# Decoder self attention on one core: four key blocks of each of 22 units are transposed by VectorE and a DRAM round trip instead of by TensorE, and the steps of the units around them are put in other orders

## The chip, the cores and the metric

One core of a Trainium2 chip runs the whole program. The metric is the device time of one execution in microseconds (us), the median of several runs. All data is float32.

The engines are named as in the profile: PE is TensorE (matrix multiplications and transposes), PEld its loading of weights, DVE is VectorE, ACT is ScalarE, POOL is GpSimd, SP is SyncE, which here only issues DMA transfers. Each engine works through its own list of instructions in order, and waits on semaphores that other engines or transfers raise.

## The reference

The program is one encoder layer over a short context (2 batches of 77 rows) and one decoder layer over `x` (2 batches of 2048 rows), 512 channels, 16 heads of 32 channels. The change concerns the causal self attention of the decoder alone:

```
yn = _ln(y, dec_n1_s, dec_n1_b)
q, k, v = heads of yn @ w.T + b                      # 16 heads of 32
scores = einsum('bhqd,bhkd->bhqk', q, k) / sqrt(32)
scores = scores + bias[None]                         # relative bias, -inf above the diagonal
attn = softmax(scores, axis=-1)
out = einsum('bhqk,bhkd->bhqd', attn, v)
y = y + out @ w_out.T + b_out
```

Behind it come cross attention over the encoder's output and a feed-forward part of width 2048. The relative bias is constant for keys that lie 127 and more behind the query, and drops out of the softmax there, so only the last two key blocks of a row take a bias.

## The kernel before, in words

The 2048 query rows of a batch `b` are cut into four blocks `m` of 512, a block into four tiles `t` of 128; the 16 heads are cut into four groups `g` of four heads. A **unit** is `(b, m, g, t)`: one tile of 128 queries for four heads `r`. It attends to `4 m + t + 1` key blocks `k` of 128 keys. "Second blocks" are the units with `m == 1`: 16 in each batch, with 5 to 8 key blocks, so that the first four key blocks are those of `m == 0`.

What is done for a unit:

- `scores`: for a piece of up to four key blocks, four matmuls (L375), one a head, write 128 queries by up to 512 keys to PSUM. The four run side by side, since each uses 32 rows of the array. VectorE moves them to the SBUF tile `pp` and takes the maximum of each row on the way (L384; with the bias for the last two key blocks L391). Behind the last piece VectorE reduces the maxima to `nm` (L401) and puts four exponentials on a list.
- `exps(1)` lets ScalarE do the next exponential of that list (L406): one for each head, over all key blocks of the unit.
- `turn`: the probabilities lie with the queries on the partitions, and the next product needs the keys there. For one key block, PE transposes four 128 by 128 tiles (L417, one a head) into one PSUM bank, and ScalarE (L423) or VectorE (L421) copies the bank to one of the eight places of the SBUF tile `pts`.
- `values`: for each key block four matmuls (L441) with the transposed probabilities as the moving operand and `vv` as weights, side by side, summed up in one PSUM bank; when the unit is closed, ScalarE copies the sum to `oT` (L454), or VectorE adds it there (L456) where the unit was summed in two parts.

The order is written out by hand. For each unit with `m > 0` there is a string of steps, which the loop over the units plays: `a` and `d` turn the next key block (with the copy on ScalarE or VectorE), `E` is one exponential of the unit that comes next, `S` the next piece of scores (of a unit up to two further on), `v` and `V` the value products of what is turned so far (`V` closes the sum), `j` and `J` a part or all of the work that other stages of the program put in between (projections, the encoder, cross attention; their PE lines are L1120, L1035, L576, L584, L748, L305, L797, L852, L860, L869). In the kernel before there are 24 strings, one for each `(b, m, t)`, the same for all four `g`. Before a unit's string starts, whatever is left of its scores and exponentials is done.

`pp` holds two units at a time, one from either end. `held_by` says which unit holds which place of it; a piece of scores may be written when its places are free, which they are when their key block has been turned.

All transfers are issued by SP, in the order of the program: loads of weights into three `wqk` buffers (L1104, L1024), large loads into `vv` (L531), rows of `x`, the bias. An issue waits for the buffer that it overwrites, and what is behind it waits too.

Of the kernel before, what the change touches and what calls it, by code (L numbers as in the profile page):

```python
# [17 lines left out]
P = 128  # L18
# [36 lines left out]
def tile_encoder_decoder(ctx: ExitStack, tc: tile.TileContext, ins, out):  # L55
# [103 lines left out]
    with (  # L159
# [17 lines left out]
        count = {"pts": 0, "oT": 0, "mm": 0}  # L177
# [178 lines left out]

        def scores(n, k0, kn):
# [23 lines left out]
            for r in range(HC):  # L381
                p, s, c = st["p"][r], banks[r].rearrange("p (k x) -> p k x", x=P), col
                if far:
                    nc.vector.tensor_scalar(  # L384
                        p[:, k0 : k0 + far], s[:, :far], 1.0, None, ALU.mult, ALU.max,
                        accum_out=st["mx"][:, r, c : c + 1],
                    )
                    c += 1
# [23 lines left out]
        def turn(load, by):  # L412

            pt = bank()
            pts = in_turn("pts", pts_all).rearrange("p (x q) -> p x q", q=P)
# [13 lines left out]
        def values(n, ks, ends, closes):  # L429
# [9 lines left out]
            for k in ks:  # L439
                for r in range(HC):  # L440
                    nc.tensor.matmul(  # L441
                        ot[rows4(r)], vv[:, k, ts(g * HC + r, HD)], got.pop((n, k, r)),
                        start=k == ks[0] and (whole or not begun), stop=k == ks[-1] and (whole or not keep),
                    )
# [1280 lines left out]
        def cross(x):  # L1725
# [127 lines left out]
        turned_to, scored_to, at = {n: 0 for n in range(end)}, {n: 0 for n in range(end)}, [0]  # L1853
        held_by = {}


        SCRIPTS = {
# [24 lines left out]
        }  # L1882

        def script_of(n):

            b, m, g, t = units[n]
            if n < end - 2:
                return SCRIPTS[b, m, t].split()
# [15 lines left out]
        def may_score(ahead=0):  # L1904

            if at[0] + ahead >= len(stream):
                return False
            n, k0, kn = stream[at[0] + ahead]
# [133 lines left out]
```

## Time and profile before

| | |
|---|---|
| median of 3 runs | 2707.5 us (2707.0 to 2708.48) |
| the profiled execution | 2708.39 us; its span 2706.3 us |
| PE busy | 2684.3 us, 99% of the span |
| DVE, ACT, POOL busy | 1848.9, 1526.2, 1002.3 us |
| granted TensorE clock | 0.998 |
| DMA | 385.10 MB, mean 142 GB/s |

Busy time of PE is the time in which at least one matmul is under way, and matmuls overlap: the mean of one (276 ns for a transpose) is its passage through the array, not what it adds. What one adds is read from the starts of neighbouring rows of the timeline. The second blocks lie between 160 and 372 us in the first batch and between 975 and 1165 us in the second. In the trace a float32 matmul makes two records, a transpose one; the program's order, shown below, counts instructions.

### The profile page before, as it was taken

To read this page: it belongs to the slowest core of one execution; us is meant where nothing else is said; L and a number is where in the kernel's file an instruction comes from. 1 tells how busy PE (TensorE), PEld (TensorE's weight loads), DVE (VectorE), ACT (ScalarE), POOL (GpSimd) and SP (SyncE) were. 2 spreads that over 40 slices of the span, in tenths; PEclk is the share of its full clock that TensorE was granted. 3 is DMA by queue.
4 is the path that set the end of the run, shared out by engine and by line. 5 is a ranking of instruction groups with operands and counts; after the bars stand their busy time and mean duration, and the time that the engine had idled before them with its cause. 6 is when DMAs were issued, how large, how long until landed. Compare 5 with 4: busy or idle time off the path is not lost.

```text
span 2706.3 us, 68257 instructions
## 1 busy us (share of the span) xinstructions
PE 2684.3 (99%) x26606; PEld 2199.2 (81%) x26606; DVE 1848.9 (68%) x5448; ACT 1526.2 (56%) x2960; POOL 1002.3 (37%) x844
## 2 busy tenths in 40 slices
PE   9999999999999999999999999999999999999998
PEld 6678777777776677778777887999999898989898
DVE  4776688888885687788888883737464746464635
ACT  3545567767886557777767794444443444444431
POOL 2602235500300513223300103556565555556546
PEclk9999999999999999999999999999999999999999
DMA  8734445511213522343311216565658565657575
GB/s 235 215 99 131 128 146 174 169 59 43 64 49 87 144 80 81 111 126 118 107 53 40 73 59 196 176 211 172 215 169 241 172 215 171 215 170 216 153 222 186
DMA packets 296276, 385.10 MB, mean 142 GB/s; under 512 B 41184, under 2 KB 165648, under 8 KB 295826
## 3 DMA queue, kind: packets, MB, share of 16 engines
q1 hardware_dynamic: 295954, 380.73, 46.9%
q8 instruction: 211, 3.46, 0.5%
q14 instruction: 111, 0.91, 0.1%
HBM read 334.15 MB, written 46.47 MB: 141 GB/s over the span
## 4 chain that ended last, share of the span: by engine, by line
PE 96%; DVE 1%; ACT 1%; DMA 1%; POOL 1%; SPq 0%; issue 0%; DVEq 0%; POOLq 0%; ACTq 0%
PE psum L417 18%; PE psum L1636 15%; PE psum L1665 13%; PE psum L375 11%; PE psum L441 9%; PE psum L1120 8%; PE psum L1799 3%; PE psum L1756 3%; PE psum L1035 3%; PE psum L852 2%; PE psum L822 1%; PE psum L860 1%; PE psum L576 1%; PE psum L797 1%; PE psum L239 1%; PE psum L215 1%
## 5 line engine op out<-in xcount | busy, mean ns | idle before, releaser
L406 ACT ACTIVATE pp<-pp,nm 128x128 f32<-128x128 f32 (+15 forms) x512 | 611.4, 1200 | 23.4 <-DVE nm L401 23.2
L384 DVE TENSOR_SCALAR_CACHE_REDUCE pp<-psum 128x512 f32<-128x512 f32 (+3 forms) x1024 | 556.7, 590 | 69.2 <-PE psum L375 67.1
L423 ACT COPY pts<-psum 128x512 f32<-128x512 f32 x696 | 374.4, 593 | 346.3 <-PE psum L417 309.5
L417 PE MATMUL psum<-ident,pp 128*128 128x128 f32 x4352 | 527.4, 276 | 5.7 <-ACT nT L310 4.0
L417 PEld LDWEIGHTS psum<-ident,pp 128*128 128x128 f32 x4352 | 475.2, 141 | 64.5 <-issue 21.4
L441 PEld LDWEIGHTS psum<-pts,vv 128*32 128x32 f32 x8704 | 225.7, 110 | 119.4 <-DVE pp L384 49.3
L375 PE MATMUL psum<-kT,q 32*128 32x512 f32 (+3 forms) x2560 | 320.3, 565 | 2.2 <-ACT kT L231 1.4
L421 DVE COPY pts<-psum 128x512 f32<-128x512 f32 x392 | 257.7, 686 | 84.8 <-PE psum L417 81.3
L1665 PE MATMUL psum<-pp 128*128 128x128 f32 x2560 | 304.5, 276 | 1.9 <-POOL pp L948 1.6
L1665 PEld LDWEIGHTS psum<-pp 128*128 128x128 f32 x2560 | 296.3, 192 | 8.6 <-issue 2.8
L441 PE MATMUL psum<-pts,vv 128*32 128x128 f32 x8704 | 278.0, 275 | 1.1 <-DVE pp L384 0.8
L948 POOL TENSOR_TENSOR pp<-pp 128x512 f32<-128x512 f32 x159 | 212.8, 1355 | 110.2 <-ACT pp L800 45.4
L1636 PE MATMUL psum<-vv,pp 128*128 128x256 f32 x1024 | 236.2, 381 | 0.0
L1636 PEld LDWEIGHTS psum<-vv,pp 128*128 128x128 f32 x1024 | 190.3, 190 | 25.8 <-issue 0.5
L391 DVE CUSTOM_DVE_ANT_0 pp<-psum,bias 128x256 f32<-128x256 f32 (+1 forms) x512 | 196.0, 411 | 13.2 <-PE psum L375 12.7
L375 PEld LDWEIGHTS psum<-kT,q 32*128 32x128 f32 x2560 | 127.5, 183 | 87.3 <-issue 50.0
L1649 DVE TENSOR_TENSOR kT<-kT,psum 128x512 f32<-128x512 f32 x96 | 65.8, 686 | 191.1 <-PE psum L1636 190.9
L1652 ACT ACTIVATE kT<-kT,vecs 128x256 f32<-128x256 f32 x192 | 86.9, 501 | 156.6 <-DVE kT L1649 155.9
L1636 PE MATMUL psum<-nT,pp 128*128 128x256 f32 x768 | 174.1, 380 | 0.0
L1636 PEld LDWEIGHTS psum<-nT,pp 128*128 128x128 f32 x768 | 144.2, 190 | 20.3 <-issue 1.6
L1673 ACT COPY oT<-psum 128x128 f32<-128x128 f32 x56 | 15.0, 268 | 239.1 <-PE psum L1665 239.1
L480 POOL TENSOR_TENSOR oT<-rirows,oT 128x512 f32<-128x512 f32 x30 | 38.4, 1279 | 288.6 <-DMA rirows<-rec 267.0
(272 smaller groups left out, 4108.2 us busy)
## 6 DMA issues: line engine op xcount, KB each, us to landing
pp<-w_d SPq DMA_DIRECT2D x520, 256.0 KB
pp<-in_dec_ff_wT_dram SPq DMA_DIRECT2D x112, 256.0 KB
bias<-tzg SPq DMA_DIRECT2D x128, 128.0 KB
pp<-wo_d SPq DMA_DIRECT2D x56, 256.0 KB
wqk<-in_dec_sa_in_wT_dram SPq DMA_DIRECT2D x52, 256.0 KB
wqk<-sa_q SPq DMA_DIRECT2D x84, 128.0 KB
vv<-in_enc_ff_wT_dram SPq DMA_DIRECT2D x8, 1024.0 KB
xr<-in_x_dram SPq DMA_DIRECT2D x32, 256.0 KB
```

Of the source, the lines that this page charges most:

```text
L375: nc.tensor.matmul(banks[r][:, : kn * P], q[rows4(r), ts(t, P)], kT[rows4(r), g, k0 * P : (k0 + kn) * P], start=True, stop=True,)
L384: nc.vector.tensor_scalar(p[:, k0 : k0 + far], s[:, :far], 1.0, None, ALU.mult, ALU.max, accum_out=st["mx"][:, r, c : c + 1],)
L391: nc.vector.tensor_tensor_reduce(p[:, k0 + far : i + 1], s[:, far:kn], near[:, 2 - (kn - far) :], 1.0, LOWEST, ALU.add, ALU.max, accum_out ...
L406: nc.scalar.activation(p, p, AF.Exp, bias=nm, accum_out=to)
L417: nc.tensor.transpose(pt[:, ts(x, P)], state[n]["p"][r][:, k], ident)
L421: nc.vector.tensor_copy(pts[:, : len(load), :], pt[:, :w])
L423: nc.scalar.copy(pts[:, : len(load), :], pt[:, :w])
L441: nc.tensor.matmul(ot[rows4(r)], vv[:, k, ts(g * HC + r, HD)], got.pop((n, k, r)), start=k == ks[0] and (whole or not begun), stop=k == ks ...
L948: engine.tensor_tensor(out, a, b, ALU.subtract)
L1120: nc.tensor.matmul(mm[:, ts(f, TOK)], left[:, c, ts(f, P)], right[:, c, :], start=c == 0, stop=c == 1,)
L1636: nc.tensor.matmul(mm[:, ts(f, TOK)], a[:, c, ts(f, P)], b[:, c, :], start=fresh and f == 0 and c == 0, stop=c == 1, skip_group_check=True,)
L1665: nc.tensor.matmul(psum[:, bank_i, ts(col, P)], lhs[:, c, :], w[:, c, :], start=fresh and k in (0, 3) and c == 0, stop=c == 3, skip_group_ ...
```

## The change

For the units whose string has a `D` in it, key blocks 0 to 3 are no longer turned by PE. There are eleven such units in each batch, 22 together: all second blocks with `t` of 1, 2 and 3 except `(g, t) = (0, 1)`. For them:

- `scores` writes the first piece (key blocks 0 to 3) into `pp` with its columns in another order, the 32-column quarters `a` outermost.
- `move_out`: when all four exponentials of the unit are done, VectorE transposes the 32 by 32 squares of those four key blocks in place, in two instructions of 128 by 1024, and behind each SP issues a transfer of 512 KB to a DRAM tile (`turn0` and `turn1` in turns).
- `move_in`: four transfers of 256 KB read it back, each into 32 partitions of the upper four places of `pts`. Moving the quarters does the rest of the transpose. Where a string has `O` and `I`, these are done during the unit before, when its state allows; otherwise at the unit's start.
- `D` puts the four landed key blocks at the head of those whose values are summed next. In `values`, the moving operand is then read in four runs of 32 elements that lie 2 KB apart.
- The other key blocks of such a unit are turned by PE as before, and use the lower four places of `pts`.

The strings are now one for each `(b, m, g, t)`. Those of `m == 2` and `m == 3` are the ones of before, four times each; those of `m == 1` all differ. `may_score` no longer asks how far the unit two earlier has been turned (the places of `held_by` say it), and `S` may take a later piece of a unit first.

```diff
+        SCRIPTS = {
...
+            (0, 1, 0, 1): 'a a a a j a E S J E a O E I S V O S O I',
+            (0, 1, 0, 2): 'd d a J E S E D S S O E E I V',
...
+            (1, 1, 2, 0): 'J d S d a a d E E O S E V S O E I S I O',
+            (1, 1, 2, 1): 'a J D a O S E E V E S I',
...
+        def move_out(n):
+
+            area = far_part(n)
+            for a in (0, 2):
+                two = area[:, a : a + 2].rearrange("p a c -> p (a c)")
+                nc.vector.transpose(two, two)
+                nc.sync.dma_start(bounce[n % 2][a : a + 2].rearrange("a p c -> p a c"), area[:, a : a + 2])
+
+        def landed(n):
+            return pts_all[:, HC : 2 * HC, :] if units[n][1] == 1 else far_part(n)
+
+        def move_in(n):
+
+            for a in range(HC):
+                nc.sync.dma_start(landed(n)[rows4(a)], bounce[n % 2][a].rearrange("(a q) c -> q a c", q=RB))
+
+        def moved_tiles(n):
+            parts = landed(n).rearrange("p a (r k x) -> p r k a x", r=HC, x=RB)
+            got.update({(n, k, r): parts[:, r, k] for k in range(HC) for r in range(HC)})
+            return list(range(HC))
...
+                    to, got_s = p[:, k0 : k0 + far], s[:, :far]
+                    if k0 == 0 and moved(n):
+                        to = to.rearrange("p a (k x) -> p a k x", x=RB)
+                        got_s = got_s.rearrange("p k (a x) -> p a k x", x=RB)
...
-            to_turn = list(range(size[n]))
+            if moved(n) and n not in gone:
+                gone.add(n)
+                move_out(n)
...
+            if moved(n) and n not in come:
+                come.add(n)
+                move_in(n)
+            far = HC if moved(n) else 0
+            to_turn = list(range(far, size[n]))
...
+                elif step == "O" and n + 1 < end and moved(n + 1) and n + 1 not in gone:
+                    if scored_to[n + 1] == size[n + 1] and not any(u == n + 1 for u, _ in late_exps):
+                        gone.add(n + 1)
+                        move_out(n + 1)
...
+                elif step == "D":
+                    turned[:0] = moved_tiles(n)
+                    far = 0
```

Three places in the order of the instructions, before and after. The line numbers of the changed kernel differ: scores are L507 there, turns L555, values L580, the exponential L542, copies of a sum to `oT` L594, copies to `pts` L561, the 32 by 32 transposes L473, the transfers out L474 and in L482. Lines ahead of the new functions keep their numbers (L205, L305), and those behind `turn` are the ones of before plus 140 (L1120 is L1260, L1035 L1175, L576 L716, L860 L1000, L1024 L1164, L531 L671).

**First place: PE around the first moved unit, `(0, 1, 0, 2)`.** Before, from the values of the unit ahead of it (24 matmuls, six key blocks) to its own (28, seven key blocks):

```order
L441 MATMUL psum<-pts,vv 32x128 x24
L417 MATMUL psum<-ident,pp 128x128 x24
L375 MATMUL psum<-kT,q 128x256 x4
L417 MATMUL psum<-ident,pp 128x128 x4
L1035 MATMUL psum<-nT,wqk 128x256 x2
L1035 MATMUL psum<-xt,wqk 128x256 x2
L576 MATMUL psum<-pp,vv 128x154 x16
L375 MATMUL psum<-kT,q 128x384 x4
L441 MATMUL psum<-pts,vv 32x128 x28
```

The same stretch now:

```order
L580 MATMUL psum<-pts,vv 32x128 x24
L555 MATMUL psum<-ident,pp 128x128 x12
L1175 MATMUL psum<-nT,wqk 128x256 x2
L1175 MATMUL psum<-xt,wqk 128x256 x2
L716 MATMUL psum<-pp,vv 128x154 x16
L507 MATMUL psum<-kT,q 128x256 x4
L507 MATMUL psum<-kT,q 128x384 x4
L580 MATMUL psum<-pts,vv 32x128 x28
```

Of 28 transposes 12 are left, those of the unit's three last key blocks; the rest stands as before in nearly the same order. The first 16 of the 28 value matmuls take the moved blocks, so they are the first instructions that need them.

**Second place: ACT and SP at the same unit.** ACT now, from the first exponentials of the moved unit (they span seven key blocks, 7x128) to those of the next unit:

```order
L542 ACTIVATE pp,sums<-pp,nm 128x7x128 x2
L561 COPY pts<-psum 128x512
L542 ACTIVATE pp,sums<-pp,nm 128x7x128
L594 COPY oT<-psum 128x128
L542 ACTIVATE pp,sums<-pp,nm 128x7x128
L561 COPY pts<-psum 128x512
L542 ACTIVATE pp,sums<-pp,nm 128x8x128 x4
```

SP now, from the loads ahead of the two transfers out to the next unit's four transfers in (before, the rows with `turn` were not there):

```order
L1164 DMA wqk<-sa_q 128x256 x4
L676 DMA pp<-in_rows_dram 77x512
L474 DMA turn_109<-pp 128x2x512 x2
L482 DMA pts<-turn_109 32x4x512 x4
L1164 DMA wqk<-sa_q 128x256 x2
L205 DMA wbig<-in_dec_sa_out_wT_dram 128x4x512
L671 DMA vv<-in_enc_ff_wT_dram 128x4x512
L474 DMA turn_110<-pp 128x2x512 x2
L482 DMA pts<-turn_110 32x4x512 x4
```

The copy of a sum to `oT` (L594) is that of the unit ahead, and needs its last value matmul. The fourth exponential of the moved unit stands behind it, and the transposes on VectorE wait for that exponential. On SP the six transfers stand in one row, ahead of loads that were issued without them before.

**Third place: PE at `(1, 1, 2, 1)`,** from the values of the unit ahead (20) to its own (24). Before:

```order
L441 MATMUL psum<-pts,vv 32x128 x20
L305 MATMUL psum<-ident,xt 128x128 x4
L860 MATMUL psum<-kT,pp 32x128 x16
L417 MATMUL psum<-ident,pp 128x128 x24
L375 MATMUL psum<-kT,q 128x512 x4
L441 MATMUL psum<-pts,vv 32x128 x24
```

Now:

```order
L580 MATMUL psum<-pts,vv 32x128 x20
L507 MATMUL psum<-kT,q 128x512 x4
L555 MATMUL psum<-ident,pp 128x128 x4
L305 MATMUL psum<-ident,xt 128x128 x4
L1000 MATMUL psum<-kT,pp 32x128 x16
L555 MATMUL psum<-ident,pp 128x128 x4
L507 MATMUL psum<-kT,q 128x512 x4
L580 MATMUL psum<-pts,vv 32x128 x24
```

Here 16 transposes are gone, and a piece of scores has moved up to stand right behind the values of the unit ahead. On VectorE the four moves of that piece out of PSUM stand ahead of the two transposes of the moved unit.

More of the change, by code (lines that the diff above doesn't have):

```diff
@@ L414, in turn @@
             pt = bank()
-            pts = in_turn("pts", pts_all).rearrange("p (x q) -> p x q", q=P)
+            halved = moved(load[0][0]) and units[load[0][0]][1] == 1
+            pts = in_turn("half", pts_all[:, :HC]) if halved else in_turn("pts", pts_all)
+            pts = pts.rearrange("p (x q) -> p x q", q=P)
             for x, (n, k, r) in enumerate(load):
@@ L1904, in may_score, with pick @@
         def may_score(ahead=0):
[L1906 removed]
+            if ahead >= len(stream):
                 return False
[L1908 to L1914 removed]
+            return not any(k in held_by for k in places(*stream[ahead]))
+        def pick(upto):
+            u = stream[0][0] if stream else end
+            rest = [k for k, p in enumerate(stream[:5]) if p[0] == u]
+            if not stream or u > upto:
+                return None
+            if moved(u):
+                rest.sort(key=lambda k: stream[k][1] == 0)
+            elif stream[0][1] == 0 and len(rest) > 1 and may_score():
+                rest[:2] = rest[1::-1]
+            elif not may_score():
+                return None
+            return next((k for k in rest if may_score(k)), None)
         def score_next(ahead=0):
[L1917 removed]
+            n, k0, kn = stream.pop(ahead)
             scores(n, k0, kn)
@@ L1955, in tile_encoder_decoder @@
                     turned.append(k)
-                    assert len(turned) <= pts_all.shape[1]
+                    assert sum(k >= HC or not moved(n) for k in turned) <= (HC if moved(n) and m == 1 else 2 * HC)
                     leave(n, k)
@@ L1972, in tile_encoder_decoder @@
                     feed(turned_to[n])
[L1973 removed]
+            assert not (to_turn or turned or parts or far), (n, to_turn, turned, len(parts), far)
         xt_ring += [sb.tile([P, D], F32, name="xt", tag="xt", bufs=2) for _ in range(2)]
```

57 lines of the change are left out of this document (35 added, 22 removed), and 116 rows, old and new, of the table SCRIPTS.

## The prediction

> **What bounds the kernel now.** I read first the page's busy times and the chain of work that ended last, then the windows over the two stretches of second blocks, then the timeline of PE there.
>
> ```profile
> PE 2684.3 (99%) x26606; PEld 2199.2 (81%) x26606; DVE 1848.9 (68%) x5448; ACT 1526.2 (56%) x2960; POOL 1002.3 (37%) x844
> PE 96%; DVE 1%; ACT 1%; DMA 1%; POOL 1%; SPq 0%; issue 0%; DVEq 0%; POOLq 0%; ACTq 0%
> 160.00:372.00 212.00, 211.51 (x2151) 167.85 (x2150) 150.81 (x533) 114.81 (x240) 50.29 (x41) 1.00 0.40 123
> 975.00:1165.00 190.00, 190.00 (x2042) 146.67 (x2041) 143.62 (x492) 130.41 (x275) 55.60 (x47) 1.00 0.33 96
> ```
>
> The chain is PE for 96%. In the windows the columns are length, then busy time of PE, PEld, DVE, ACT, POOL, the clock, the DMA share and GB/s. In the second blocks PE idles 0.5 us of 402, DVE is at 71% and 76%, the DMA engines at 40% and 33%. So any PE work removed there shortens the program at once, and any new wait of PE lengthens it at once: nothing hides either. Everything else is to be measured against PE's own pace.
>
> **What is removed.** The timeline of PE from the end of one unit's values to the next unit's turns, in the first batch:
>
> ```profile
> 185.91 3.21 PE L417 MATMUL psum<-ident,pp 128*128 128x128 f32 x24
> 189.15 0.71 PE L375 MATMUL psum<-kT,q 32*128 32x256 f32 x8
> 189.79 0.66 PE L417 MATMUL psum<-ident,pp 128*128 128x128 f32 x4
> 190.29 1.03 PE L1035 MATMUL psum<-nT,wqk 128*128 128x256 f32 x4
> 191.15 1.03 PE L1035 MATMUL psum<-xt,wqk 128*128 128x256 f32 x4
> 192.02 4.36 PE L576 MATMUL psum<-pp,vv 128*128 128x154 f32 x32
> 196.31 0.93 PE L375 MATMUL psum<-kT,q 32*128 32x384 f32 x8
> 197.17 1.74 PE L441 MATMUL psum<-pts,vv 128*32 128x128 f32 x56
> 198.84 2.84 PE L417 MATMUL psum<-ident,pp 128*128 128x128 f32 x24
> 201.60 0.71 PE L375 MATMUL psum<-kT,q 32*128 32x256 f32 x8
> ```
>
> 24 transposes take 201.60 - 198.84 = 2.76 us, 0.115 each. The change takes away 22 units x 4 key blocks x 4 heads = 352 of them: 352 x 0.115 = **40.5 us less on PE**. The value matmuls stay in number. Their operand now comes in four runs of 32 elements; the nearest row is their own:
>
> ```profile
> L441 PE MATMUL psum<-pts,vv 128*32 128x128 f32 x864 | 27.1, 275 | 0.4 <-DVE pp L384 0.3
> L421 DVE COPY pts<-psum 128x512 f32<-128x512 f32 x40 | 26.7, 686 | 11.4 <-PE psum L417 11.4
> L423 ACT COPY pts<-psum 128x512 f32<-128x512 f32 x65 | 35.2, 592 | 23.3 <-PE psum L417 21.1 <-DVE nm L401 1.0 <-ACT pts L423 0.9
> L384 DVE TENSOR_SCALAR_CACHE_REDUCE pp<-psum 128x512 f32<-128x512 f32 x60 | 37.8, 687 | 11.7 <-PE psum L375 11.7
> L470 DVE STREAM_TRANSPOSE rt<-ri 128x32 f32<-128x32 f32 x4 | 0.8, 212 | 0.1
> L558 DVE TENSOR_SCALAR pp<-pp,emv,ers 77x512 f32<-77x512 f32 x2 | 1.0, 538 | 0.0
> ```
>
> 27.1 us for 864 records, two to an instruction, is 0.063 us each. Between nothing and twice that, the new operand costs 0 to 352 x 0.063 = 22 us; I take 0, since as many columns pass as before. The 88 copies of turned banks that fall away (58 of ACT, 30 of DVE by the two orders) are 34 and 21 us off the path.
>
> **What is added on VectorE.** 44 transposes of 128 by 1024. A 128 by 32 one took 0.212 us, and 512 elements read from SBUF took 0.538, or 1.05 ns an element: one costs between 1024 x 1.05 ns = 1.08 us and 32 x 0.212 = 6.8 us. I take 0.212 + 992 x 1.05 ns = 1.25 us, next to the rows with long operands. The 55 us in all fit into DVE's idle 24 to 29% there. The moves into `pp` in another column order I cost as L384 is; twice that would be 88 x 0.69 = 61 us, on DVE too. Cover: PE has PSUM banks for two pieces of scores ahead; without it, what stands behind the transposes in DVE's queue (moves of scores, copies of turned blocks) stops PE.
>
> **What is added in waiting.** This decides. In none of the 22 units does the order let the transposes on VectorE begin before PE is at the values of the unit ahead (or at the scores right in front of them): an exponential stands behind that unit's copy to `oT`, or the transposes stand behind moves of later scores. From there the unit needs, one after the other, the exponential, two transposes, two transfers out, four in. PE meanwhile has only the work that stands up to the first moved value matmul.
>
> First place, `(0, 1, 0, 2)`: PE's cover is 12 transposes, 1.38; L1035, 192.02 - 190.29 = 1.73; L576, 4.29; scores of 256 and 384 keys, 0.64 and 0.86: 8.9 us. What it must cover:
>
> ```profile
> 177.94 1.05 ACT L406 ACTIVATE pp<-pp,nm 128x896 f32<-128x896 f32 x1
> 178.97 1.04 ACT L406 ACTIVATE pp<-pp,nm 128x896 f32<-128x896 f32 x1
> 186.04 0.27 ACT L454 COPY oT<-psum 128x128 f32<-128x128 f32 x1 [3.90 <-PE psum L441]
> 186.60 2.05 ACT L423 COPY pts<-psum 128x512 f32<-128x512 f32 x4 [0.29 <-PE psum L417]
> ```
>
> The values ahead ended at 185.91; ACT is through the copy and free at 186.60, 0.69 later; an exponential of seven key blocks takes 1.03 and the two transposes 2.5: 4.2 us. Then the transfers. The trace has no DRAM round trip of this size, but it has loads of 256 KB that an engine waited for:
>
> ```profile
> 0.72 0.38 SPq L275 DMA_DIRECT2D xt<-in_x_dram  x1
> 3.49 0.69 DVE L282 BATCH_NORM_STATS2 bnst<-xt 128x6 f32<-128x512 f32 x1 [2.57 <-DMA xt<-in_x_dram]
> 275.11 0.91 SPq L262 DMA_DIRECT2D xr<-in_x_dram  x2
> 278.41 1.27 POOL L1090 TENSOR_TENSOR xr<-xr,row_dec_sa_out_b 128x512 f32<-128x512 f32 x1 [0.25 <-DMA xr<-in_x_dram]
> 1090.79 0.97 SPq L262 DMA_DIRECT2D xr<-in_x_dram  x2
> 1095.69 1.28 POOL L1090 TENSOR_TENSOR xr<-xr,row_dec_sa_out_b 128x512 f32<-128x512 f32 x1 [7.41 <-DMA xr<-in_x_dram]
> ```
>
> From issue to use: 2.8 us in an empty queue, 3.3 and 4.9 with others in flight. Behind the second transpose come one landing out (512 KB, the first 512 KB being 1.25 ahead), two more issues (0.91 for two) and one landing in. At least 2.8 + 2.8 = 5.6, at most 4.9 + 4.9 = 9.8; I take 3.3 + 0.9 + 3.3 and 0.2 for the handings over, **7.7 us**. The first unit then needs 4.2 + 7.7 = 11.9 against 8.9: PE stands for 3.0 us, more than the 16 x 0.115 = 1.8 that it saved.
>
> Third place, `(1, 1, 2, 1)`:
>
> ```profile
> 318.11 1.14 PE L375 MATMUL psum<-kT,q 32*128 32x512 f32 x8
> 319.18 1.95 PE L441 MATMUL psum<-pts,vv 128*32 128x128 f32 x64
> 1019.87 1.08 PE L860 MATMUL psum<-kT,pp 77*32 77x128 f32 x32
> 1020.88 1.35 PE L1035 MATMUL psum<-xr,wqk 128*128 128x256 f32 x5
> ```
>
> Cover: two pieces of scores at 1.07, L860 1.01, eight turns 0.92 and four at L305 as dear as turns, 0.46: 4.5 us. The transposes stand behind the four moves of the first of these pieces: 1.07 + some 2.6 (four at up to 0.69, overlapping) + 2.5 = 6.2 us, then 7.7. PE stands for 9.4.
>
> The same for all: PE's cover from the unit ahead's last value matmul is, in order of time, 8.9, 11.2, 11.3, 6.1, 13.4, 9.1, 10.4, 11.2, 7.0, 7.0, 7.9 in the first batch and 6.2, 7.9, 8.8, 6.8, 13.0, 4.5, 11.1, 6.9, 7.4, 6.5, 9.4 in the second. The second transpose ends 2.4 to 4.6 after that point (2.9 where VectorE's own addition to `oT` stands ahead, 4.2 behind a copy and one exponential, 7.0 at the sixth with four exponentials, 6.2 and 6.3 at two units with a piece of scores ahead). In six units the transposes hang on a point ahead of the previous stall, which then counts as cover. Shortfalls at 7.7: 3.0, 0, 0, 4.5, 0, 5.6, 0.2, 0, 3.1, 0.8, 2.1, together 19.3; and 5.7, 0, 2.9, 3.8, 0, 9.4, 2.9, 5.1, 2.7, 1.7, 2.9, together 37.1. **56.4 us more.** With 5.6 the sum is 29, with 9.8 it is 87.
>
> **The queue of SP.** Six issues in a row wait on VectorE and on landings, and loads of weights stand behind them; three units have a 1 MB load to `vv` just ahead.
>
> ```profile
> SPq L1104 <- PE psum L1120: 341.8, 57, 17.5
> GB/s 235 215 99 131 128 146 174 169 59 43 64 49 87 144 80 81 111 126 118 107 53 40 73 59 196 176 211 172 215 169 241 172 215 171 215 170 216 153 222 186
> ```
>
> SP's time is mostly waiting for PE to free a buffer, so it has room; at the 235 GB/s of the busiest early slice 1 MB takes 4.5 us, so these three units lose 0 to 13 us. I take 4. The 46 MB that are added (44 x 0.5 MB and 88 x 0.25) meet engines at 33 to 40%.
>
> **Sum.** 2708.4 (the profiled execution, 0.9 above the median of the runs) - 40.5 + 56.4 + 4 = **2728 us**. The stretches of other blocks have the same order as before.
>
> **Rivals.** *The round trip is quick enough.* If the two landings with the issues between take 4.7 us in place of 7.7, the shortfalls sum to 18 and the time is 2708 - 40.5 + 18 = 2686. For it: most of the 2.8 us may be a fixed part, that the first 512 KB have behind them; DVE, ACT and SP all get time while PE stands. Against it: no row has a landing below 2.8. It decides below 6.3 us, where shortfalls equal 40.
>
> *The round trip is dear.* At 9.8 us the time is 2708 - 40.5 + 87 = 2755. For it: two units' worth of loads in flight, as at 1090.79. [...]
>
> *It does not do what it says:* steps `O` and `I` are to start the move a unit ahead. `O` does nothing while an exponential of that unit is left, so a move a full unit early does not occur; were it so, the full 40.5 would be gained, 2668. The order speaks against it.
>
> **How the numbers follow.** The forecast (shortfalls of 46 to 75) 0.46, quick 0.32, dear 0.14, balance between quick and forecast 0.08. A measurement here tells about 0.2%, 5.4 us. Faster takes the quick case and a little of the balance, 0.34; the same 0.10; slower 0.56. The range reaches from 2682 (quick) to 2764 (dear, with the queue); the forecast's own is 2712 to 2748.
>
> **What would show it.** PE's idle time in the two stretches, released by transfers from `turn` to `pts`, should be some 56 us at 22 places, longest at `(1, 1, 2, 1)`; transposes on VectorE 1.25 us each; 4000 turns left. Right steps and a wrong sum would mean that 7.7 is off. The prediction is wrong if PE finds the moved blocks landed, or if PE waits for something else, such as late weights or PSUM banks.

## The result: slower, and by more than predicted

The changed kernel takes 2776.2 us (2774.0 to 2777.7), the kernel before 2707.8 (2707.0 to 2708.5): a ratio of 1.0252 with a 95% interval of 1.0234 to 1.0270, 68.5 us more. The prediction was 2728, with a range to 2764.

The page of the changed kernel, busy times and the chain of waits:

```profile
span 2775.7 us, 67709 instructions
PE 2679.0 (97%) x26254; PEld 2181.8 (79%) x26254; DVE 1879.0 (68%) x5466; ACT 1498.8 (54%) x2902; POOL 1002.1 (36%) x844
PE 87%; DMA 6%; DVE 4%; ACT 1%; issue 1%; POOL 1%; SPq 1%; DVEq 0%; POOLq 0%; ACTq 0%
L555 PE MATMUL psum<-ident,pp 128*128 128x128 f32 x4000 | 494.4, 278 | 10.5 <-ACT pp L542 6.0
L580 PE MATMUL psum<-pts,vv 128*32 128x128 f32 x8704 | 290.0, 281 | 63.1 <-DMA pts<-turn 49.7
```

The same two groups in the page of the kernel before:

```profile
L417 PE MATMUL psum<-ident,pp 128*128 128x128 f32 x4352 | 527.4, 276 | 5.7 <-ACT nT L310 4.0
L441 PE MATMUL psum<-pts,vv 128*32 128x128 f32 x8704 | 278.0, 275 | 1.1 <-DVE pp L384 0.8
```

PE was in the chain for 96% and is now for 87%; transfers and VectorE have come in. 352 turns are gone (4352 to 4000). PE idles 2775.7 - 2679.0 = 96.7 us, against 22.0 before, and of the 74.7 us that are new, 62.0 stand ahead of the value matmuls (63.1 in L580 against 1.1). But PE's busy time, which should have fallen by 40.5, fell by 5.3. The windows over the second blocks of both batches (length, then busy time of PE, PEld, DVE, ACT, POOL, the granted clock, the DMA share and GB/s):

```profile
164.00:393.00 229.00, 194.59 (x1888) 151.32 (x1890) 157.22 (x517) 98.81 (x206) 38.57 (x31) 0.96 0.70 208
1008.00:1236.00 228.00, 184.10 (x1871) 134.70 (x1860) 161.18 (x508) 113.82 (x237) 50.51 (x43) 0.90 0.59 172
```

Before, the clock was 1.00 in both and the DMA share 0.40 and 0.33. What PE waited for, in us in all, times, and the longest:

```profile
PE psum L580 <- DMA pts<-turn: 49.7, 12, 10.9
PE psum L1175 <- DMA wqk<-sa_q: 7.3, 2, 4.5
PE psum L555 <- ACT pp L542: 6.0, 9, 0.9
PE psum L580 <- DVE mx L527: 4.5, 2, 3.4
PE psum L580 <- DVE pp L473: 4.1, 1, 4.1
```

**The round trip.** The timelines of VectorE, of SP's queue and of PE for the first two moved units: start, duration, what.

```profile
187.84 2.36 DVE L473 STREAM_TRANSPOSE pp<-pp 128x1024 f32<-128x1024 f32 x2
189.10 1.50 SPq L474 DMA_DIRECT2D turn<-pp  x2
191.98 2.12 SPq L482 DMA_DIRECT2D pts<-turn  x4
199.27 3.00 PE L580 MATMUL psum<-pts,vv 128*32 128x128 f32 x56 [4.09 <-DVE pp L473]
197.96 2.36 DVE L473 STREAM_TRANSPOSE pp<-pp 128x1024 f32<-128x1024 f32 x2
199.22 1.49 SPq L474 DMA_DIRECT2D turn<-pp  x2
207.59 2.01 SPq L482 DMA_DIRECT2D pts<-turn  x4
214.52 1.96 PE L580 MATMUL psum<-pts,vv 128*32 128x128 f32 x64 [1.03 <-DMA pts<-turn]
```

From the end of the second transpose (190.20) to the first moved value matmul it is 9.1 us, and 14.2 in the second case, where 2 MB of weights stood in the queue just ahead. PE stood for 1.0 us or more ahead of the moved values at 17 places; there the way was 8.4 to 14.2 us long, 10.2 in the mean (the difference of such rows). The prediction took 7.7. The difference lies in the way in: from the second transpose to the first issue of the way in it is 3.1 us in the mean, where the prediction took 3.3, but from there to the value matmul 7.1 (6.6 to 8.2), where it took 0.9 + 3.3 + 0.2 = 4.4. At the place predicted to be the longest, `(1, 1, 2, 1)`, the windows of the way in, each 1 us:

```profile
1138.00:1139.00 1.00, 0.00 (x0) 0.00 (x0) 0.00 (x0) 0.00 (x0) 1.00 (x2) 0.50 1.07 209
1139.00:1140.00 1.00, 0.00 (x0) 0.00 (x0) 0.00 (x0) 0.00 (x0) 0.92 (x2) 0.50 1.03 211
1140.00:1141.00 1.00, 0.00 (x0) 0.00 (x0) 0.00 (x0) 0.00 (x0) 1.00 (x1) 0.50 1.04 229
```

All sixteen DMA engines are full (shares of 1.03 to 1.07) at 209 to 229 GB/s (289 and 328 in the windows on either side) while every other engine but POOL stands. Two stores (`y<-xr`) were issued at 1137.42, so some of the bytes may be theirs; at the first moved unit, with only loads issued behind the way in, it is 196 to 227 GB/s at 1.00 to 1.07, from 195 to 198 us. At the rate of the three windows above 1 MB is some 4.8 us: the four loads of 256 KB share the engines, and the price of a single load of 256 KB, 3.3 us, on which the prediction built, isn't theirs. Nor are the loads alike. Weights that are loaded to all 128 partitions fill the engines too, but at nearly twice the rate, 387 GB/s in this window of the same run:

```profile
203.00:204.00 1.00, 1.00 (x11) 1.00 (x10) 0.23 (x1) 0.97 (x2) 0.00 (x0) 1.00 1.06 387
```

The loads that the prediction took its price from go to 128 partitions as well, while each transfer of the way in lands on 32.

**A lower clock behind a stand.** PE at the same place, and then windows of 2 us:

```profile
1130.42 1.14 PE L507 MATMUL psum<-kT,q 32*128 32x512 f32 x8
1142.47 2.79 PE L580 MATMUL psum<-pts,vv 128*32 128x128 f32 x48 [10.91 <-DMA pts<-turn]
1145.19 2.09 PE L507 MATMUL psum<-kT,q 32*128 32x512 f32 x8
```

```profile
1132.00:1134.00 2.00, 0.00 (x0) 0.00 (x0) 2.00 (x12) 2.00 (x5) 0.68 (x1) 0.94 1.06 409
1134.00:1136.00 2.00, 0.00 (x0) 0.00 (x0) 0.92 (x6) 0.20 (x2) 1.92 (x3) 0.50 0.72 280
1144.00:1146.00 2.00, 2.00 (x28) 1.32 (x24) 0.00 (x0) 0.69 (x2) 2.00 (x3) 0.50 0.00 0
1148.00:1150.00 2.00, 2.00 (x12) 1.30 (x10) 1.97 (x9) 0.00 (x0) 0.00 (x0) 1.00 0.00 0
```

Some 2 us after PE stopped (1131.56) the granted clock is halved, and it is back only 5 us after PE began again (0.59 from 1147.0 to 1147.5, then 1.00). The same piece of scores takes 2.09 us in place of 1.14. A shorter stand lowers the clock too: behind the one of 3.08 us that ends at 1161.25, the window from 1162 to 1164 has a clock of 0.50. Behind the stand of 1.03 us that ends at 214.52 it stays at 1.00. The prediction did not weigh the clock.

### The profile page after: what moved, and what is told of

Its sections match the earlier page's. It is cut to its first block, busy times and chain, and to the rows that moved or that the text cites. A ratio compares the mean times of both kernels' runs of the same rounds, so it can differ in the third digit from the quotient of the medians.

```text
span 2775.7 us, 67709 instructions
## 1 busy us (share of the span) xinstructions
PE 2679.0 (97%) x26254; PEld 2181.8 (79%) x26254; DVE 1879.0 (68%) x5466; ACT 1498.8 (54%) x2902; POOL 1002.1 (36%) x844
## 4 chain that ended last, share of the span: by engine, by line
PE 87%; DMA 6%; DVE 4%; ACT 1%; issue 1%; POOL 1%; SPq 1%; DVEq 0%; POOLq 0%; ACTq 0%
PE psum L555 16%; PE psum L1776 14%; PE psum L1805 12%; PE psum L507 9%; PE psum L580 9%; PE psum L1260 7%; PE psum L1939 3%; PE psum L1896 3%; DMA turn<-pp 2%; PE psum L1175 2%; PE psum L992 2%; DMA pts<-turn 2%; PE psum L962 1%; DVE pp L473 1%; PE psum L1000 1%; DVE pp L520 1%
## 5 line engine op out<-in xcount | busy, mean ns | idle before, releaser
L542 ACT ACTIVATE pp<-pp,nm 128x128 f32<-128x128 f32 (+15 forms) x512 | 611.6, 1200 | 49.9 <-DVE nm L537 42.8
L561 ACT COPY pts<-psum 128x512 f32<-128x512 f32 x638 | 344.3, 593 | 344.1 <-PE psum L555 316.3
L555 PE MATMUL psum<-ident,pp 128*128 128x128 f32 x4000 | 494.4, 278 | 10.5 <-ACT pp L542 6.0
L555 PEld LDWEIGHTS psum<-ident,pp 128*128 128x128 f32 x4000 | 442.0, 142 | 70.9 <-issue 25.2
L580 PEld LDWEIGHTS psum<-pts,vv 128*32 128x32 f32 x8704 | 234.4, 112 | 182.8 <-issue 81.1
L580 PE MATMUL psum<-pts,vv 128*32 128x128 f32 x8704 | 290.0, 281 | 63.1 <-DMA pts<-turn 49.7
L507 PE MATMUL psum<-kT,q 32*128 32x512 f32 (+3 forms) x2560 | 327.8, 569 | 1.5 <-DVE kT L1290 0.5
L559 DVE COPY pts<-psum 128x512 f32<-128x512 f32 x362 | 237.3, 684 | 81.6 <-PE psum L555 79.4
L507 PEld LDWEIGHTS psum<-kT,q 32*128 32x128 f32 x2560 | 132.4, 184 | 89.8 <-issue 49.0
```

What stands on the lines that cost most here:

```text
L507: nc.tensor.matmul(banks[r][:, : kn * P], q[rows4(r), ts(t, P)], kT[rows4(r), g, k0 * P : (k0 + kn) * P], start=True, stop=True,)
L542: nc.scalar.activation(p, p, AF.Exp, bias=nm, accum_out=to)
L555: nc.tensor.transpose(pt[:, ts(x, P)], state[n]["p"][r][:, k], ident)
L559: nc.vector.tensor_copy(pts[:, : len(load), :], pt[:, :w])
L561: nc.scalar.copy(pts[:, : len(load), :], pt[:, :w])
L580: nc.tensor.matmul(o if len(p.shape) == 2 else o.rearrange("p (a x) -> p a x", x=RB), vv[:, k, ts(g * HC + r, HD)], p, start=k == ks[0] an ...
```

## The experiments

Three theories were on the table. A: TensorE stands for the transfers and works at a lower clock behind each stand. B: the new orders of the steps themselves cost. C: the value matmuls are dear with a strided operand. Each run is compared with the kernel before on the same chip.

| run | us | against before | first batch | second batch |
|---|---|---|---|---|
| before | 2706.1 to 2707.8 | | 207.7 | 186.6 |
| the change | 2776.2 | +68.5 | 229.8 | 228.1 |
| e1_orders_alone | 2750.6 | +42.9 | 217.4 | 206.5 |
| e2_no_transfers | 2691.5 | -16.2 | 193.3 | 177.5 |
| e9_no_move | 2688.3 | -17.8 | 191.0 | 174.9 |
| e14_old_order_no_move | 2688.9 | -17.7 | 188.7 | 179.8 |
| e10_in_alone | 2716.2 | +10.1 | 208.1 | 189.5 |
| e4_filled | 2772.9 | +65.3 | 229.3 | 226.6 |
| e3_wide_in | 2977.7 | +270.0 | 331.6 | 324.2 |
| e8_direct | 2845.8 | +138.6 | 253.7 | 268.4 |
| e5_old_order_free | 2733.5 | +26.4 | 210.8 | 200.7 |
| e6_old_order | 2765.8 | +58.6 | 221.3 | 225.1 |
| e7_old_order_direct | 2871.2 | +164.0 | 275.9 | 277.1 |
| e11_two_heads | 2739.3 | +33.2 | 220.7 | 205.4 |
| e12_chosen_units | 2703.7 | -2.8 | 202.3 | 186.3 |
| e13_chosen_four | 2733.0 | +26.4 | 207.9 | 201.6 |
| e15_eight_units | 2705.4 | -0.8 | 202.3 | 186.8 |

The last two columns are from each profiled execution: from the last value matmul ahead of the second blocks to their own last one.

### Orders alone, and no transfers

```diff
# e1_orders_alone
-                    turned[:0] = moved_tiles(n)
+                    for k in range(HC):
+                        turn([(n, k, r) for r in range(HC)], "ad"[k % 2], HC + k)
+                        leave(n, k)
+                    turned[:0] = range(HC)
# e2_no_transfers
-                nc.sync.dma_start(bounce[n % 2][a : a + 2].rearrange("a p c -> p a c"), area[:, a : a + 2])
...
-                nc.sync.dma_start(landed(n)[rows4(a)], bounce[n % 2][a].rearrange("(a q) c -> q a c", q=RB))
```

> The orders of the change without the move: where `D` stands, TensorE turns the four key blocks and ACT and VectorE copy them, as before; no block goes through DRAM and the scores are put down plainly. Theory A (TensorE stands for the transfers, and behind a stand it works at a lower clock for a while): the 352 transposes come back and the stands of the transfers go, so 2700 to 2722 us, with a granted clock of 1.00 in the windows of the second blocks. Rival B (the new orders themselves cost: late exponentials, weights, PSUM banks): 2735 us or more. Rival C (the strided operand makes the value matmuls dear): as A here, since the operand is plain again.

> The changed kernel with its 44 transposes on VectorE, its orders and its strided operand, but without the transfers out and in (the values read what the upper places of `pts` happen to hold; that part of the computation is left out). A: both the stands and the lower clock go, which leaves 2708 - 40.5 and the small new waits (exponentials 6, weights about 4): 2668 to 2685 us, clock 1.00. B: 2700 or more, since the orders are the same. C (the 35 us of extra TensorE work come from the strided operand): the stands of some 50 us go, the 35 stay, 2705 to 2720, with 56 records of L580 taking well over 1.74 us without a stand ahead.

e1 gave 2750.6 (ratio 1.0157, 1.0140 to 1.0174), e2 2691.5 (0.9942, 0.9927 to 0.9957). Without transfers the loss is gone: the transfers cost 68.5 + 16.2 = 84.7 us. The page of e2:

```profile
span 2688.4 us, 67435 instructions
PE 2657.4 (99%) x26254; PEld 2165.9 (81%) x26254; DVE 1875.6 (70%) x5466; ACT 1496.8 (56%) x2902; POOL 1001.1 (37%) x844
```

From this trace to that of the change, PE's idle time grows by 65.7 us (31.0 to 96.7) and its busy time by 21.6 (2657.4 to 2679.0). But e2 is 24 above 2708 - 40.5 = 2667 and 6.5 above the top of A's range, and e1 is on B's side. e1 says less than it seems to: with the turns at `D`, four in a row just ahead of their use, PE waits 6 us for copies and 15 for late exponentials in the two batches. The order was not made for such turns.

### What the 24 us are

```diff
# e9_no_move: e2_no_transfers, and
-                nc.vector.transpose(two, two)
# e14_old_order_no_move: the same with the orders of before, less four turns a unit
+            (0, 1, 0, 2): 'E d d S d E J E E S S O D V I S',
```

> The changed kernel without transfers and without the 44 transposes on VectorE (the moved blocks are not turned at all; the value matmuls read what `pts` holds; that part of the computation is left out). TensorE's instructions, their order and the strided operand stay. e2_no_transfers, with the transposes, came out at 2691.5, 24 us above 2708 - 40.5. If the transposes in VectorE's queue make the 24 us: 2665 to 2675. If the new orders of scores and exponentials make them, or the strided operand: 2685 to 2692, as with the transposes.

> The orders of before, less the four turns of each of the 22 units, with neither transposes on VectorE nor transfers (that part of the computation is left out), the value matmuls in their places. If the 40.5 us are there to be had and e9_no_move lost 21 of them by its new order: 2665 to 2672 us. If taking the turns away leaves TensorE waiting for VectorE and ACT whatever the order: 2680 to 2692.

2688.3 (0.9929, 0.9914 to 0.9944) and 2688.9 (0.9934, 0.9921 to 0.9948). So neither the 44 transposes (e2 less e9: 1.6 us, inside the intervals) nor the new order is it: **taking 40.5 us of turns off PE is worth 18 us, in either order.** C falls with it, as a value row of e9 with its strided operand shows; the same row took 1.74 before.

```profile
192.51 1.74 PE L577 MATMUL psum<-pts,vv 128*32 128x128 f32 x56
```

The batches say where. In e14 the first one is 19.0 us shorter, nearly all of 11 x 1.84 = 20.2. The second is 6.8 shorter. There, in e14 and then in the kernel before, by line and form over the second batch:

```profile
L577 PE MATMUL psum<-pts,vv 128*32 128x128 f32 x848 | 29.2, 276 | 3.4 <-DVE pts L556 3.3
L504 PE MATMUL psum<-kT,q 32*128 32x256 f32 x64 | 9.5, 426 | 0.0
```

```profile
L441 PE MATMUL psum<-pts,vv 128*32 128x128 f32 x821 | 25.8, 274 | 0.0
L375 PE MATMUL psum<-kT,q 32*128 32x256 f32 x64 | 6.9, 426 | 0.0
```

Values now wait for VectorE's copies (3.3 us, ten times), and the same 64 records of scores stretch from 6.9 to 9.5 us without a recorded wait: rows overlap, so a wait that is shorter than one passage (426 ns) counts as busy. Counted from each start to the next, over the second blocks of the second batch, scores take 41.5 us in e14 against 35.0 before, values 28.7 against 24.9, and the turns that are left 0.125 us each against 0.115. That is nearly all of the missing 13 us (20.2 - 6.8). The semaphores in the traces say for whom PE waits: starts of PE that follow a release by VectorE within 0.15 us lie 18.6 us in all behind the start ahead of them, against 7.9 before, and those that follow ScalarE 3.6 against 2.8. So with the turns gone, VectorE's queue, at 76% before, is next there. Unit by unit, the second batch of e14 gains 1.3 to 2.0 us where `t` is 3, and loses 0.4 to 1.1 where `t` is 1. In e9, with the new order, it is ScalarE's releases that grow (10.5 against 2.8; VectorE's 8.5). Outside these second blocks e14's trace is 4.7 us longer than that of before. Waits for exponentials right behind them, 2.7 us against 1.3, are a part of it; the rest the runs don't settle.

### The way in alone

```diff
+                if (n % 2, a) not in sent:
+                    sent.add((n % 2, a))
                     nc.sync.dma_start(bounce[n % 2][a : a + 2].rearrange("a p c -> p a c"), area[:, a : a + 2])
```

> The changed kernel with the way out written only once for each of the two DRAM buffers, so that the way in waits for no way out (the values of all but the first two moved units are wrong for that reason; this leaves out 20 of the 22 ways out). Bounded by 2691 (no transfers) and 2776 (both). If each way costs in proportion to its part of the chain, out 3 to 5 us and in 7, a third to a half of the 85 us goes: 2735 to 2748. If the bytes decide (half of them gone), more than half: 2705 to 2730. If the landing place that the values ahead still hold is what delays the way in, little goes: 2755 or more.

2716.2 (1.0031, 1.0018 to 1.0043): of the 84.7 us, 58 go with the way out, more than its share of the chain (3.1 of 10.2 us). The bytes are halved, and the way in no longer waits for exponentials and transposes either; the run doesn't part the two. What is left, 26 us, is a way in of some 7 us that can't start before the values ahead are done with its landing place (in 19 of the 22 units its first issue comes within 0.1 us of their end). The waits that the profile puts down to transfers:

```profile
PE psum L584 <- DMA pts<-turn: 9.5, 2, 5.6
PE psum L1179 <- DMA wqk<-sa_q: 5.8, 2, 4.7
```

### Is the clock the price?

```diff
+            if moved(n) and 0 in ks:
+                for _ in range(int(max(0, STALL.get(units[n], 0) - 0.5) / 0.115)):
+                    nc.tensor.transpose(psum[:, ring[0], :P], ident, ident)
```

> The changed kernel, but TensorE turns the identity into a spare PSUM bank (never read) just ahead of the first moved value matmul, in each unit for 0.5 us less than it stood there in the trace, 54 us in all. A (the clock drops because TensorE stands): the fill takes the place of the stand, the clock stays at 1.00 and the 35 us of slower work go, so 2735 to 2750 us. C (the strided operand is what is slow): the time stays at 2770 to 2785. B says nothing of it. If the fill were simply added, 2830.

2772.9 (1.0239, 1.0223 to 1.0254): 3 us, not 35. The time is one that C had named, but C said that the strided values stay slow, and they don't: the clock did what A said. The place of the 10.91 us stand:

```profile
1134.73 10.04 PE L587 MATMUL psum<-ident 128*128 128x128 f32 x90
1144.70 1.52 PE L591 MATMUL psum<-pts,vv 128*32 128x128 f32 x48
1146.15 1.14 PE L507 MATMUL psum<-kT,q 32*128 32x512 f32 x8
```

The values behind the fill take 1.52 us in place of 2.79, the scores 1.14 in place of 2.09. The whole account, from the page of this run:

```profile
span 2772.0 us, 68609 instructions
PE 2719.1 (98%) x26708; PEld 2221.5 (80%) x26708; DVE 1877.2 (68%) x5466; ACT 1497.7 (54%) x2902; POOL 1001.1 (36%) x844
```

The fill is 454 turns, 52.2 us. PE's other work is 2719.1 - 52.2 = 2666.9, down by 12.1; standing and fill together are 52.9 + 52.2 = 105.1, up by 8.4 from 96.7. PE works faster and then stands longer. I read this so: in this order each unit's end is set by its transfers, and slower work of PE lies inside that time. The fill is a part of the test only, since the mean granted clock of the run rose from 0.985 to 0.993, against 0.998 before. The lower clock is real, and taking away more than half of it gained 3 us; so it is hardly on the path. That was a miss of theory A, which added it to the stands.

### The ways of the bytes

```diff
# e3_wide_in
-                nc.sync.dma_start(landed(n)[rows4(a)], bounce[n % 2][a].rearrange("(a q) c -> q a c", q=RB))
+                nc.sync.dma_start(landed(n)[:, a], bounce[n % 2][:, rows4(a)])
# e8_direct: none out, and
+                for j in range(HC):
+                    nc.sync.dma_start(landed(n)[rows4(a), j], far_part(n)[rows4(j), a])
```

> Each of the four transfers in lands on all 128 partitions (one of the four blocks of 512 columns) in place of 32 partitions with all their columns; bytes, number and order as in the changed kernel. If 32 partitions are a narrow door, the way in falls from about 7 us to 5 or less, 17 stands lose some 2 us each and some of them fall below the length at which the clock drops: 2715 to 2750 us. If the way in is made of issues and a fixed part, it stays at about 7 us and the time at 2770 to 2780.

> The changed kernel, orders and all, with the same 16 direct transfers of 64 KB in place of the way out and in. From the second transpose it takes 16 issues, 7.2 us, and a landing of about 2, against the 10 to 12 that the round trip took: the stands fall by 1 to 3 us each and with them part of the time at the lower clock, 2730 to 2760 us. If queues and fixed parts decide it stays at 2776 or grows.

Both are far slower: 2977.7 (1.0999, 1.0982 to 1.1015) and 2845.8 (1.0508, 1.0492 to 1.0524). In e3, while PE stands for a way in:

```profile
1320.00:1321.00 1.00, 0.00 (x0) 0.00 (x0) 0.00 (x0) 0.00 (x0) 0.00 (x0) 0.50 0.27 104
1321.00:1322.00 1.00, 0.00 (x0) 0.00 (x0) 0.00 (x0) 0.00 (x0) 0.00 (x0) 0.50 0.26 100
```

A share of 0.26 is as much as four of sixteen engines, at half of the 209 to 229 GB/s above. The outermost dimension of this source is the four quarters; the change's way in, with 32 outermost, has a share of 1.03 to 1.07, and weights that land on 128 partitions as e3's transfers do have 1.06. What e3 has alone is the four, so I put the low share down to it; no run varied that by itself. So e3's time tells of the low share first. Its windows tell of the 32 partitions as well: with the same bytes from the same DRAM tile, but landing on 128 partitions, it moves 100 GB/s at a share of 0.26, an estimated 385 at a share of 1 (100 / 0.26), near the weights' 387 at 1.06. The change's way in has 209 at 1.07, some half of that. This speaks for the narrow door that e3 was to test; a way in to 128 partitions at a full share was not run. In e8 the bytes are halved, and SP needs longer to issue them:

```profile
191.22 10.13 SPq L482 DMA_DIRECT2D pts<-pp  x16
```

0.63 us each, where I had taken 0.45 (the landing of about 2 was an estimate of mine too; at the change's first moved unit the first issue in comes 1.8 us behind the second transpose, 190.20 to 191.98); the 16 issues are as long as the whole round trip was, and scores wait until their place in `pp` has been read out (VectorE's moves of scores wait for these transfers for 38.2 us between 160 and 400 us).

### Starting the move earlier

In the orders of before, four exponentials of a unit are done in the unit ahead, so the move can begin nearly a unit earlier. e5 and e6 do that, with the moved value matmuls last; e5 has no transfers, e7 the direct ones.

```diff
+            (0, 1, 0, 2): 'E d d S d E J E E O S S D V I S',
...
-                    turned[:0] = moved_tiles(n)
+                    turned += moved_tiles(n)
```

> The orders of before in the second blocks, less the four turns of each of the 22 units; the transposes on VectorE stand a unit early (behind the last exponential, ahead of the last scores and the values of the unit ahead), the moved value matmuls stand last among the values; no transfers (that part of the computation is left out). e2_no_transfers came out 24 us above 2708 - 40.5 = 2667. If the new orders are what costs those 24 us: 2667 to 2675 us here. If the transposes themselves do it (2.5 us of VectorE in front of moves of scores and copies): 2685 to 2695 here too.

> The same with the transfers through DRAM: out a unit early, in as soon as the values ahead are done. Cover of the way in is then nearly a whole unit (8.6 us less a part of the values) against some 7 us. If the stands come from the late start of the move: 2670 to 2700 us, faster than before. If it is the bytes (2 MB more in each 8.6 us are 240 GB/s beside the 123 GB/s that run there already, and busy slices carry 235 to 280): TensorE stands in many units, 2730 us or more.

> As e6_old_order, but the blocks go from SBUF to SBUF in 16 transfers of 64 KB when the values ahead are done, with none through DRAM: half the bytes, and 16 issues at 0.45, 7.2 us of SP's queue, in each unit. If bytes decide, less than e6_old_order by some tens of us. If the issues of SP decide (7.2 and a landing of some 2 against a cover of 8), 2690 to 2720 and late weights behind them in the queue.

2733.5 (1.0093, 1.0076 to 1.0110), 2765.8 (1.0214, 1.0198 to 1.0229), 2871.2 (1.0604, 1.0588 to 1.0619). e5 and e7 lie above all that was expected, and e6 in the range of its rival, 2730 or more. The transfers now cost e6 - e5 = 32 us in place of 84.7. That fits a lack of cover, though e5 waits for VectorE already, and such waits cover transfers too. But the transposes, which cost 1.6 us in the changed order, cost 44 here (e5 against e14, which also has the step `O` behind the last scores). They stand in VectorE's queue ahead of the moves of scores. Two rows of VectorE and two of PE in e5:

```profile
199.33 2.36 DVE L473 STREAM_TRANSPOSE pp<-pp 128x1024 f32<-128x1024 f32 x2
227.71 2.36 DVE L473 STREAM_TRANSPOSE pp<-pp 128x1024 f32<-128x1024 f32 x2
202.47 1.38 PE L505 MATMUL psum<-kT,q 32*128 32x256 f32 x8
230.19 2.26 PE L505 MATMUL psum<-kT,q 32*128 32x512 f32 x8
```

The scores take 0.71 and 1.14 where nothing waits. So the place in the changed order was the better one for VectorE and the worse one for the transfers.

### A smaller move

e11 moves two of the four heads: one transpose on VectorE, half the bytes each way, and stands between the last scores and the values ahead (`O` in front of `V`).

```diff
+            area = far_part(n)[:, :, : HM * P]
+            nc.vector.transpose(area, area)
+            nc.sync.dma_start(bounce[n % 2].rearrange("a p c -> p a c"), area)
```

> A smaller move in the orders of before: only heads 0 and 1 of the four far key blocks are moved (one transpose of 1024 elements on VectorE, 512 KB out, 512 KB in), heads 2 and 3 are turned by TensorE, two blocks of each to a bank. The transpose stands behind the moves of the last scores and ahead of the values of the unit ahead; the way in starts when these are done; the moved value matmuls come last. It takes 22 x 8 x 0.115 = 20 us off TensorE. If the bytes and the place in VectorE's queue were the trouble, the cover (about 8.5 us) holds against a way in of some 5: 2688 to 2700 us, faster than before. If any transpose in VectorE's queue holds up scores by its whole length, or the way out and in still takes 10 us or more: 2710 to 2740.

2739.3 (1.0119, 1.0104 to 1.0134). That is above the expected 2688 to 2700, in its rival's range. Unit by unit its trace gave 0.8 to 0.9 us in nine units, nearly all of 8 x 0.115 = 0.92, and lost up to 7 us in others. The next runs kept only units that gained; e13 moves all four heads there.

> The move of e11_two_heads in nine units only, those that were each 0.8 to 0.9 us shorter in its trace than in that of before: (0, 1, 0, 3), (0, 1, 1, 1), (0, 1, 1, 3), (0, 1, 2, 2), (0, 1, 2, 3), (0, 1, 3, 3), (1, 1, 0, 3), (1, 1, 1, 3), (1, 1, 2, 3); the others are those of before. If a unit with cover gains its full saving, 9 x 8 x 0.115 = 8.3 us: 2699 to 2702. If those gains were only made up from stands ahead of them: 2706 to 2712.

> The same nine units with all four heads moved (two transposes, 512 KB out twice, 256 KB in four times), 9 x 1.84 = 16.6 us off TensorE. If the cover of a whole unit ahead of a moved one holds against 10 to 12 us out and in: 2691 to 2698. If it does not, stands of 2 us or more at some of the nine eat it up: 2700 to 2712.

> e12_chosen_units without the move of (1, 1, 2, 3), which stands behind the one unit that had a new loss of 1.2 us there, (1, 1, 2, 2), and two ahead of (1, 1, 3, 3) with 2.1. If that move's transfers or its transpose made these losses: about 3 us less than e12_chosen_units, 2699 to 2702 us, faster than before by more than 0.2%. If they come from the order of scores at the start of the second batch or from elsewhere: 2703 to 2707.

e12 took 2703.7 (0.9990, 0.9981 to 0.9999), e13 2733.0 (1.0093, 1.0078 to 1.0108), e15 2705.4 (0.9999, 0.9990 to 1.0008). The time of e12 lies between its two ranges. Its chosen units kept 0.7 to 0.9 us each, so a unit with cover does gain nearly its full saving; 2.8 us less in all is about what can be told from no change, and in e15 the loss at `(1, 1, 2, 2)` and `(1, 1, 3, 3)` stayed without the move that I suspected. e13 came out above its expectations, with losses of up to 6.4 us in single units; what makes them stays open. No version here is clearly better than the kernel before.

## Why the prediction was wrong, step by step

The direction held and the size did not: +20 predicted, +68.5 measured. By terms:

| term | predicted | measured | by |
|---|---|---|---|
| turns taken off PE | -40.5 | -17.8 | e9 and e14 |
| transposes on VectorE | 0 | +1.6 | e2 less e9 |
| transfers and SP's queue | +60.4 | +84.7 | the change less e2 |

- **The first failed step is "any PE work removed there shortens the program at once".** It was drawn from 0.5 us of idle time of PE in 402. The turns did go (their group fell by 38.4 us in e9), but another limit lay close behind, in the old order VectorE's queue in the second batch, and it shows mostly in rows that count as busy. This is 22.7 of the 48.6 us that were missed.
- **The second is the mis-sized "7.7 us" for the transfers.** They took 10.2 in the mean, above the upper bound of 9.8. The sum of shortfalls that the prediction gave for 9.8 was 87; the transfers cost 84.7. The mis-sized part is the way in, 7.1 us in place of 0.9 + 3.3 + 0.2 = 4.4; the way out, 3.1, was priced about right. The price was that of a single load of 256 KB to 128 partitions, while here 1 MB comes in at once, in pieces that land on 32 partitions and keep the engines busy nearly twice as long for the same bytes (209 to 229 GB/s against the weights' 387).
- **The places were right.** I had named stands of 3.0, 4.5, 5.6 and 9.4 us at `(0, 1, 0, 2)`, `(0, 1, 1, 2)`, `(0, 1, 2, 1)` and `(1, 1, 2, 1)`; the trace has 4.1, 7.5, 3.8 and 10.9, the last the longest, as said. In all they were 61.9 us, at 17 places, against 56.4. That they were not longer, with a way of 10.2, fits what e4 showed: behind a stand PE works slower (2.09 us for 1.14 of scores), and slower work is cover.
- **The lower clock was not foreseen.** The prediction costed all of PE's work at the pace of before. Taking more than half of it away gained 3 us (e4), so this is hardly what broke the sum.
- **Transposes on VectorE** took 1.18 us each (2.36 for two) against 1.25. They cost next to nothing where the change puts them, as taken, and 44 us where e5 puts them: the cover that the prediction named, PSUM banks for two pieces of scores, was not enough there.
- **The strided operand** costs nothing, as taken. **Late weights** were 7.3 us at two places, against 4.
- Of the rivals, the quick round trip is out, and the dear one was right on the transfers, 9.8 us against 10.2. Loads in flight, its reason, show at the second moved unit, 14.2 us; the windows of e3 and of the weights speak for the 32 partitions as a further one. That steps `O` and `I` begin the move a full unit early did not occur, as said; e6 shows what it would have been worth, and at what price on VectorE.

## What to carry to other kernels

An engine that is busy for 99% of a stretch isn't proof that its work sets the pace: rows that overlap hide waits shorter than one passage (426 ns here), so take the work out once, with nothing put in its place, before building what replaces it. Price a chain of transfers by all its bytes, at the rate that transfers of the same shape have, not by one load of another shape (here 10.2 us in place of 7.7). A slower clock behind a stand cost little here (3 us, e4), where the next wait covered it.

## What the runs showed of the hardware

- At the longest stand, 10.91 us, the granted clock fell to 0.50 some 2 us into it and was back 5 us after work began; the same matmuls took nearly twice as long in between (2.09 against 1.14 us). It fell to 0.50 at a stand of 3.08 us too, and stayed at 1.00 at one of 1.03 (the change).
- A transfer whose outermost dimension was 4 ran at a DMA share of 0.26 and about 100 GB/s, one with 32 outermost at 1.03 to 1.07 and 209 to 229 GB/s (e3 against the change).
- At a full DMA share, weights came in to 128 partitions at 387 GB/s and the windows of the way in to 32 partitions had 209 to 229 (the change; e3's 100 GB/s at a share of 0.26 is an estimated 385 at a share of 1).
- An issue on SP took 0.63 us for 64 KB from SBUF to SBUF (e8), and about 0.5 for 256 KB from DRAM (2.12 us for four).
- A moving operand in four runs of 32 elements was as fast as one run of 128 (1.74 us for 56 records in e9 and before).
- VectorE transposed 128 by 1024 elements in squares of 32 in 1.18 us (2.36 for two, the change).
